# Attention's first norm: the weight multiplied straight out of PSUM, squares in place, the row's scale put on afterwards by ScalarE

## The chip, the cores and the metric

The kernel runs on one core of a Trainium2 chip. The metric is the device time of one execution in microseconds (us); lower is better. Before the change it is 8548.28 us, the median of three executions (8543.92 to 8550.57).

## The reference

Two layers are computed on `x`, fp32 of 8 images x 192 channels x 64 x 64 pixels. The first is a selective scan over the image in four directions, with a norm and a projection at its end; the second is window attention in 8 x 8 windows with a top-16 mask, followed by a feed-forward part. Cut to the part that matters here:

```python
# end of layer 0
y = layernorm2d(y, ln_w, ln_b)
y = grn(y, grn_gamma, grn_beta)
x = conv1x1(y, W_out)                       # 384 -> 192 channels
# start of layer 1
xs = transpose(x)                           # tokens x 192
shortcut = _layer_norm(xs, norm1_g, norm1_b)  # (x-mu)*rsqrt(var+1e-5)*g + b
qkv = windows(shortcut) @ qkv_w.T + qkv_b
...                                         # top-16 softmax in windows, proj
x2 = shortcut + out
hdn = _layer_norm(x2, norm2_g, norm2_b)
x2 = x2 + gelu(hdn @ fc1_w.T + fc1_b) @ fc2_w.T + fc2_b
```

## The kernel before

Three strands of work are laid out for each image: a *front* (projection and 3x3 convolution, `front`), the *scan* (`scan`: eight steps, each over four directions and three blocks of 128 channels) and the *window rows* (`window_row`: eight rows of windows, 512 tokens each). While image b is scanned, the front of image b+1 and the window rows of image b-1 run beside it. At the start there is only a front and a scan without window rows; at the end eight window rows run after the last scan.

The order on each engine is not the order of the code. Every piece of work is handed to a planner, `plan(engine, cost, function, r=..., w=...)`, with a cost in ns, what it reads and what it writes. `Plan.order` (L146) then runs a list scheduler over all of them twelve times, with ranks by due time, keeps its best outcome, and emits the instructions of PE (TensorE), ScalarE (ACT), VectorE (DVE), GpSimd (POOL) and the transfer queue SP in that order. A changed piece of work or cost therefore gives a new order everywhere. Lanes (`plan.lane`) keep the order in which pieces of one strand may take buffers.

PSUM has two banks for the scan's `nb` and six that all else shares (`l_ps`, L450, handed out by `bank()`, L466). Each unit of the scan takes three of the six for its gates (`g`, matmuls at L673; read by ScalarE's Abs at L730 and by VectorE's multiplies at L722, L737 and L739) and four more for its outputs (read at L828 and L833). The window rows take theirs from the same six.

A window row begins thus. `zg`, the scan's result for 512 tokens, is loaded (L1027) and scaled by ScalarE (L1032). For each half `t2` of the row a bank `pz` gets two blocks of 128 tokens x 192 channels by the matmuls of L1047 (`tokens`); the mean over the channels has been taken out of `w_out` beforehand, so only the scale remains of the norm. ScalarE squares each block out of PSUM with the sum along the row accumulated into `ss`, and writes the squares themselves, which nobody reads, into `s0` (L1053). GpSimd turns the sum into the mean plus 1e-5 (L1062); `rsqrt` (L469) makes 1/sqrt of it with Ln, Exp and Square on ScalarE (L478 to L480) and three steps on GpSimd (L483 to L485). Then VectorE multiplies each block in PSUM by the row's scale `ss` and by the weight `n1_g` and writes it to `s0` in SBUF (L1069). That ends the use of `pz`. The bias of the norm has been folded into later weights.

`s0` is transposed by PE (L1012), copied to `sT` (L1020) and projected to q, k and v (L1093, L1131); it is read once more when the residual is added (L1368), a multiply-free twin of the new instruction in shape: 128x384 out of PSUM with a second operand from SBUF. Further names used below: the top-16 search (L1234 to L1238), the exps and shares of the softmax (L1276, L1288), the second norm's scaling (L1411), fc1 (L1443, L1447), its bias (L1454), gelu over a whole row with an activation-table load before and after (L1463, L1464), and fc2 (L1477).

Of the kernel before, what the change touches and what calls it, by code (L numbers as in the profile page):

```python
# [25 lines left out]
AF = mybir.ActivationFunctionType  # L26
ALU = mybir.AluOpType
# [4 lines left out]
P = 128  # L32
B, DM, H, W = 8, 192, 64, 64
# [16 lines left out]
def view(ap, dims, offset=0):  # L50

    return bass.AP(ap.tensor, ap.offset + offset, [ap.ap[0]] + dims)
# [231 lines left out]
def tile_ss2d_then_window_attention(ctx: ExitStack, tc: tile.TileContext, a: dict, out: bass.AP):  # L284
# [6 lines left out]
    nc = tc.nc  # L291
# [7 lines left out]
    def load(name, src=None, rows=None):  # L299

        nonlocal n_loads
        src = a[name] if src is None else src
        shape = list(src.shape)
        t = const.tile([rows or shape[0]] + shape[1:], F32, tag=name, name=name)
        if rows:
            nc.vector.memset(t[HALF:rows], 0.0)
        queues[n_loads % 2].dma_start(t[0 : shape[0]], src)
        n_loads += 1
        return t
# [18 lines left out]
    n1_g = load("n1_g", a["n1_g"].partition_broadcast(P))  # L328
# [41 lines left out]
    with tc.tile_pool(name="prep", bufs=2) as prep, tc.tile_pool(name="prep_ps", bufs=2, space=PSUM) as prep_ps:  # L370
# [12 lines left out]
        for n, pair in enumerate(PAIRS):  # L383
            for k, (d, _) in enumerate(pair):
                w = w_g2[64 * k : 64 * k + 64, n * P : (n + 1) * P]
# [51 lines left out]
        for ci in range(2):  # L437
            w = w_f1[:, ci, :]
# [15 lines left out]
    plan = Plan()  # L454
    vec = lambda n: (n / 0.96 + 69, 88)
# [10 lines left out]
    def bank(name="lp"):  # L466
        return Held(l_ps, [P, 512], name, tag="lp")

    def rsqrt(v, key, shape, name, gain=1.0):  # L469

        c = (gain / 2) ** (1 / 3)
        if gain not in log_c:
            log_c[gain] = blank(f"log_c{len(log_c)}", [P, 1], math.log(c))
        r, sq = Held(small, shape, name + "_r"), Held(small, shape, name + "_q")
        plan("ACT", tiny, lambda: nc.scalar.activation(r(), v(), AF.Ln), r=[key], w=[r])  # L478
        plan("ACT", tiny, lambda: nc.scalar.activation(r(), r(), AF.Exp, scale=-0.5, bias=log_c[gain]), w=[r])
        plan("ACT", tiny, lambda: nc.scalar.activation(sq(), r(), AF.Square), r=[r], w=[sq])  # L480

        def newton():
            nc.gpsimd.tensor_mul(v(), v(), sq())  # L483
            nc.gpsimd.tensor_scalar(v(), v(), -1.0, 3.0 * c * c, ALU.mult, ALU.add)
            nc.gpsimd.tensor_mul(v(), v(), r())  # L485

        plan("POOL", (750.0, 60.0), newton, r=[r, sq], w=[key])
# [516 lines left out]
    def window_row(b, g, z, sc, bb):  # L1004
# [30 lines left out]
        s0 = Held(lpool, [P, NT, DM], "s0", bufs=2)  # L1035
        for t2 in range(2):
            pz = bank()
            ss = Held(small, [P, 2], "ss")
            for k in range(2):

                def tokens(t2=t2, k=k, pz=pz):
                    tt = 2 * t2 + k
                    for ct in range(CT):
                        for w in range(2):
                            half = pz()[64 * w : 64 * w + 64, k * DM : (k + 1) * DM]
                            tok = view(zg(), [[CH, 64]], ct * 512 + 2 * tt + w)
                            nc.tensor.matmul(half, lhsT=tok, rhs=w_out[:, ct, :], start=ct == 0, stop=ct == CT - 1)  # L1047

                plan("PE", mm(3, DM), tokens, r=[zg], w=[(pz, k), (s0, "room")])
                plan(  # L1050
                    "ACT",
                    (430.0, 100.0),
                    lambda k=k, pz=pz, ss=ss, t2=t2: nc.scalar.activation(  # L1053
                        s0()[:, 2 * t2 + k, :], pz()[:, k * DM : (k + 1) * DM], AF.Square, accum_out=ss()[:, k : k + 1]
                    ),
                    r=[(pz, k)],
                    w=[(s0, t2), (ss, k)],
                )
            plan(
                "POOL",  # L1060
                tiny,
                lambda ss=ss: nc.gpsimd.tensor_scalar(ss(), ss(), 1.0 / DM, 1e-5, ALU.mult, ALU.add),  # L1062
                w=[ss],
            )
            rsqrt(ss, ss, [P, 2], "ss")

            def scaled(t2=t2, pz=pz, ss=ss):
                for k in range(2):
                    nc.vector.scalar_tensor_tensor(  # L1069
                        s0()[:, 2 * t2 + k, :],  # L1070
                        pz()[:, k * DM : (k + 1) * DM],
                        ss()[:, k : k + 1],
                        n1_g,
                        ALU.mult,
                        ALU.mult,
                    )

            plan("DVE", (650.0, 90.0), scaled, r=[pz, ss], w=[(s0, t2)])
            yield
        plan.lane = 7  # L1080
        two_blocks(sT, "sT", s0)
# [5 lines left out]
        for tt in range(NT):  # L1087
            pq = bank()

            def projected(tt=tt, pq=pq):  # L1090
# [11 lines left out]
                r=[pq],  # L1102
                w=[(qk, tt)],
# [5 lines left out]
                r=[(qk, tt)],  # L1109
                w=[pq],  # L1110
# [7 lines left out]
                r=[pq],  # L1118
                w=[(nn, tt)],
# [4 lines left out]
        for p2 in range(2):  # L1124
            pv = bank()

            def values(p2=p2, pv=pv):
# [18 lines left out]
                r=[pv],  # L1146
                w=[(v, p2)],
# [13 lines left out]
            w=[nn],  # L1161
# [12 lines left out]
        for k in range(4):  # L1174
            pt = bank()

            def turn(k=k, pt=pt):
# [10 lines left out]
                r=[pt],  # L1188
                w=[(qkT[k // 2], k % 2)],
# [26 lines left out]
        for r in range(3):  # L1216
# [5 lines left out]
                r=[pas[r]],  # L1222
                w=[(at, r)],
            )
        for r in range(3):
# [21 lines left out]
            def mask(rng=rng, less=less):  # L1247
# [9 lines left out]
            part = lambda rng=rng: at()[:, rng, :]  # L1257
# [6 lines left out]
                w=[(at, r)],  # L1264
# [5 lines left out]
                r=tops,  # L1270
                w=[(down, r)],
# [24 lines left out]
        for r in range(3):  # L1296
            pt = bank()

            def turn(r=r, pt=pt):
# [11 lines left out]
                r=[pt],  # L1311
                w=[(at, r)],
# [18 lines left out]
        for w in range(2):  # L1331
# [7 lines left out]
                r=[po[w]],  # L1339
                w=[("oT", w)],  # L1340
# [6 lines left out]
        for t2 in range(2):  # L1347
            pp = bank()
            two = slice(2 * t2, 2 * t2 + 2)
            stats, mv, sd = Held(small, [P, 2, 6], "stats"), Held(small, [P, 2, 2], "mv"), Held(small, [P, 2], "sd")  # L1350

            def projected(t2=t2, pp=pp):
# [20 lines left out]
                r=[pp, s0],  # L1373
                w=[(x2, t2)],
            )

            def moments(t2=t2, stats=stats, mv=mv):
# [9 lines left out]
                r=[mv],  # L1387
                w=[sd],
# [8 lines left out]
                r=[mv],  # L1397
                w=[less_m],
# [5 lines left out]
                r=[sd],  # L1404
                w=[less_m],
# [31 lines left out]
        for m2 in range(NM // 2):  # L1437
# [12 lines left out]
            for k in range(2):  # L1450
# [6 lines left out]
                    r=[ph[k]],  # L1457
                    w=[(hd, 2 * m2 + k)],
# [10 lines left out]
        for ci in range(2):  # L1469
# [4 lines left out]
            def narrowed(ci=ci, pf=pf, n=n):  # L1474
# [22 lines left out]
                r=[pf],  # L1497
                w=[ot],
# [13 lines left out]
    def windows(b, z, made):  # L1512
        for g in range(NG):
            yield from window_row(b, g, z, *made[b])
# [107 lines left out]
```

## Time and profile before

| | |
|---|---|
| median of three executions | 8548.28 us |
| the profiled execution | 8535.73 us, of which the span is 8533.9 us |
| granted TensorE clock, mean | 0.818 |
| busy PE / DVE / ACT / POOL | 83% / 74% / 64% / 68% |
| L1053, squares (ACT), 128x192 | 256 times, 325 ns mean, 83.1 us busy |
| L1069, scaled multiply (DVE), 128x192 | 256 times, 407 ns mean, 92.1 us busy |
| L1368, residual add (DVE), 128x384 | 128 times, 547 ns mean, 69.8 us busy |

The page of the profile is that of one execution. "Busy" is the time in which an engine has an instruction under way; where two of one kind overlap it is less than count times mean. In the rows of groups, `out<-in` gives tiles by the program's names without buffer numbers (`s` is `s0`, `lp` a bank), then the shape, the count, the busy time, the mean duration of one, and the idle time of the engine just before such instructions with what ended most of it. `L1069` is line 1069 of the kernel. The chain of work that ended last is followed back from the last instruction, at each step to what released it.

### The profile page before, as it was taken

The numbers are of one execution on the slowest core, as the hardware profiler recorded it, in microseconds if no ns is written. First come the engines' busy times: TensorE is split into PE (matmuls) and PEld (weight loads), VectorE is DVE, ScalarE is ACT, GpSimd is POOL, SyncE is SP. The second block draws the span as 40 slices with busy tenths as digits, with TensorE's granted clock in tenths as the row PEclk, the third lists the DMA queues.
The fourth block names the chain that finished last, engine by engine and source line by source line (L and its number), as shares of the span: only waits on it lengthen the run. The fifth ranks groups of instructions, "written<-read, shape, count | busy, mean of one in ns | idle before, by whom it ended". The sixth has DMA issues, their size and how long they took to land.

```text
span 8533.9 us, 147117 instructions
## 1 busy us (share of the span) xinstructions
PE 7066.1 (83%) x51224; PEld 3646.0 (43%) x51224; DVE 6350.5 (74%) x15549; ACT 5425.1 (64%) x12281; POOL 5839.1 (68%) x5918
## 2 busy tenths in 40 slices
PE   5787688888888888788888888888888888888887
PEld 2333344444444444444444444444444444444554
DVE  1366778888787887877788777787788888888543
ACT  1354447676676757665676656766577656667776
POOL 0377877778777677777777667676777777777311
PEclk8887578887888889786888888977778878778888
DMA  6776154212533155213531134311211111111110
GB/s 176 188 194 160 49 137 120 79 43 72 137 98 78 36 138 133 70 47 85 147 95 51 42 88 132 107 39 46 56 44 41 46 52 53 40 41 42 26 23 12
DMA packets 1037949, 695.69 MB, mean 82 GB/s; under 512 B 704116, under 2 KB 860215, under 8 KB 1037207
## 3 DMA queue, kind: packets, MB, share of 16 engines
q1 hardware_dynamic: 1035830, 684.99, 30.1%
q8 instruction: 406, 6.65, 0.3%
q14 instruction: 337, 2.75, 0.1%
q10 hardware_dynamic: 1376, 1.30, 0.1%
HBM read 453.43 MB, written 232.67 MB: 80 GB/s over the span
## 4 chain that ended last, share of the span: by engine, by line
PE 37%; DVE 17%; ACT 17%; POOL 13%; DMA 9%; issue 5%; SPq 1%; POOLq 0%; DVEq 0%; ACTq 0%
PE g L673 10%; PE lp L560 4%; PE lp L1477 4%; PE lp L1443 3%; POOL pr L791 3%; DMA strip<-pad 3%; DMA zg<-z 3%; ACT at L1276 2%; PE lp L1093 2%; PE lp L1047 2%; ACT at L1288 2%; POOL ab L761 2%; POOL pr L776 2%; POOL dx L842 2%; DVE pr L737 2%
## 5 line engine op out<-in xcount | busy, mean ns | idle before, releaser
L673 PE MATMUL g<-xe,w_g 32*128 32x512 f32 x3648 | 1301.1, 780 | 316.3 <-DVE dx L828 115.5
L673 PE MATMUL g<-xo,w_g 32*128 32x512 f32 x3648 | 1263.1, 774 | 238.5 <-DVE dx L828 65.1
L761 POOL TENSOR_TENSOR ab<-ab 128x512 f32<-128x512 f32 x672 | 863.2, 1285 | 407.3 <-ACT ab L730 401.4
L791 POOL TENSOR_TENSOR pr<-pr,rr 128x512 f32<-128x512 f32 x672 | 873.0, 1299 | 340.9 <-ACT rr L774 307.0
L776 POOL TENSOR_TENSOR pr<-pr 128x512 f32<-128x512 f32 x672 | 872.9, 1299 | 316.5 <-DVE pr L737 204.5
L730 ACT ACTIVATE ab<-g 128x512 f32<-128x512 f32 x1344 | 770.8, 593 | 320.6 <-PE nb L673 166.2
L560 PE MATMUL lp<-strip,w_cv 128*32 128x256 f32 x9216 | 687.2, 442 | 288.4 <-DMA strip<-pad 264.5
L780 POOL TENSOR_TENSOR pr<-pr 128x512 f32<-128x512 f32 x672 | 869.9, 1295 | 24.3
L842 POOL TENSOR_TENSOR dx<-dx,hu 128x512 f32<-128x512 f32 x576 | 739.0, 1291 | 183.6 <-DVE hu L833 172.3
L673 PEld LDWEIGHTS g<-xe,w_g 32*128 32x128 f32 x3648 | 461.1, 220 | 895.4 <-DVE dx L828 242.5
L673 PEld LDWEIGHTS g<-xo,w_g 32*128 32x128 f32 x3648 | 441.8, 219 | 804.5 <-issue 202.7
L772 ACT ACTIVATE rr<-nb,eps 128x512 f32<-128x512 f32 x672 | 460.0, 685 | 486.5 <-DVE nb L769 423.9
L787 DVE SCALAR_TENSOR_TENSOR nb<-nb,rr 128x512 f32<-128x512 f32 x672 | 465.2, 692 | 338.5 <-ACT rr L774 337.2
L1477 PE MATMUL lp<-hd,w_f 128*64 128x256 f32 (+1 forms) x2304 | 603.9, 500 | 75.2 <-ACT hd L1463 61.0
L795 DVE SCALAR_TENSOR_TENSOR nb<-nb,pr 128x512 f32<-128x512 f32 x672 | 464.8, 692 | 195.6 <-POOL pr L791 191.8
L560 PEld LDWEIGHTS lp<-strip,w_cv 128*32 128x32 f32 x9216 | 314.0, 123 | 669.3 <-issue 357.6
L850 POOL TENSOR_TENSOR y<-y,dx 128x512 f32<-128x512 f32 x384 | 596.4, 1561 | 3.1
L769 DVE TENSOR_TENSOR nb<-nb,ab 128x512 f32<-128x512 f32 x672 | 465.2, 692 | 154.9 <-POOL ab L761 125.8
L752 ACT ACTIVATE nb<-nb 128x512 f32<-128x512 f32 x672 | 396.8, 591 | 221.5 <-DVE pr L737 111.3
L840 POOL TENSOR_TENSOR y<-hu,dx 128x512 f32<-128x512 f32 x192 | 248.8, 1303 | 406.6 <-DVE hu L833 406.2
L833 DVE TENSOR_TENSOR hu<-g,hid 128x512 f32<-128x512 f32 x768 | 519.9, 678 | 8.0 <-PE g L673 6.4
L673 PE MATMUL nb<-xe,w_g 32*128 32x512 f32 x672 | 497.9, 829 | 8.0 <-DVE hid L802 7.9
(201 smaller groups left out, 17042.9 us busy)
## 6 DMA issues: line engine op xcount, KB each, us to landing
strip<-pad SPq DMA_DIRECT2D x1152, 132.0 KB
xd<-xsT SPq DMA_DIRECT2D x384, 256.0 KB
pad<-xin SPq DMA_DIRECT2D x192, 264.0 KB
xs<-st SPq DMA_DIRECT2D x192, 256.0 KB
xsT<-sn SPq DMA_DIRECT2D x192, 256.0 KB
xd<-xs SPq DMA_DIRECT2D x192, 256.0 KB
x<-xs SPq DMA_DIRECT2D x64, 768.0 KB
z<-y SPq DMA_DIRECT2D x64, 768.0 KB
```

Source lines behind the costliest of these rows:

```text
L560: nc.tensor.matmul(pc()[q * RG : (q + 1) * RG, k * 256 : (k + 1) * 256].rearrange("p (h w) -> p h w", h=4), lhsT=w_cv[:, ct, q, dx, :], rh ...
L673: nc.tensor.matmul(dst, lhsT=w[rows, col : col + P], rhs=xp[rows, :], start=True, stop=True)
L730: lambda r=r: nc.scalar.activation(ab()[:, r, :], g[r](), AF.Abs),
L761: plan("POOL", gp(512), lambda: nc.gpsimd.tensor_add(ab()[:, 0, :], ab()[:, 0, :], ab()[:, 1, :]), w=[ab])
L769: plan("DVE", vec(512), lambda: nc.vector.tensor_add(nb(), nb(), ab()[:, 0, :]), r=[ab], w=[nb])
L776: plan("POOL", gp(512), lambda: nc.gpsimd.tensor_add(one(), one(), pr()[:, 1, :]), r=[(pr, 1)], w=[(pr, 0)])
L780: lambda: nc.gpsimd.tensor_add(one(), one(), pr()[:, 2, :]),
L791: plan("POOL", gp(512), lambda: nc.gpsimd.tensor_mul(one(), one(), rr()), r=[rr], w=[(pr, 0)])
L833: lambda: nc.vector.tensor_mul(like(hu(), d), like(pu(), d), state(d, ct)),
L842: plan("POOL", gp(512), lambda: nc.gpsimd.tensor_add(dx(), dx(), hu()), r=[hu], w=[dx])
L850: nc.gpsimd.tensor_add(y, y, dx().rearrange("p (c i) -> p i c", c=CH))
L1477: nc.tensor.matmul(dst[:, at : at + rhs.shape[-1]], lhsT=lhsT, rhs=rhs, **flags)
```

## The change

Three things change in each of the 128 halves. One VectorE instruction multiplies both blocks, 384 columns, by the weight as soon as the matmuls are done and writes them to `s0`. ScalarE's two squares, now one piece of work, write over the blocks in PSUM rather than into `s0`, after that multiply, and the bank is free from then on. When the scale is there, ScalarE multiplies the two blocks in `s0` by it, in place (`Copy` with a scale read from `ss`), where VectorE multiplied out of PSUM by scale and weight. The steps that make the scale are the same.

```diff
                 plan("PE", mm(3, DM), tokens, r=[zg], w=[(pz, k), (s0, "room")])
-                plan(
-                    "ACT",
-                    (430.0, 100.0),
-                    lambda k=k, pz=pz, ss=ss, t2=t2: nc.scalar.activation(
-                        s0()[:, 2 * t2 + k, :], pz()[:, k * DM : (k + 1) * DM], AF.Square, accum_out=ss()[:, k : k + 1]
-                    ),
-                    r=[(pz, k)],
-                    w=[(s0, t2), (ss, k)],
-                )
+            two = slice(2 * t2, 2 * t2 + 2)
+            plan(
+                "DVE",
+                vec(2 * DM),
+                lambda two=two, pz=pz: nc.vector.tensor_mul(
+                    s0()[:, two, :],
+                    pz()[:, 0 : 2 * DM].rearrange("p (k m) -> p k m", k=2),
+                    n1_g.unsqueeze(1).to_broadcast([P, 2, DM]),
+                ),
+                r=[pz],
+                w=[(s0, t2)],
+            )
+
+            def squares(pz=pz, ss=ss):
+                for k in range(2):
+                    part = pz()[:, k * DM : (k + 1) * DM]
+                    nc.scalar.activation(part, part, AF.Square, accum_out=ss()[:, k : k + 1])
+
+            plan("ACT", (860.0, 100.0), squares, w=[pz, ss])
             plan(
                 "POOL",
                 tiny,
@@
             rsqrt(ss, ss, [P, 2], "ss")
 
-            def scaled(t2=t2, pz=pz, ss=ss):
+            def scaled(t2=t2, ss=ss):
                 for k in range(2):
-                    nc.vector.scalar_tensor_tensor(
-                        s0()[:, 2 * t2 + k, :],
-                        pz()[:, k * DM : (k + 1) * DM],
-                        ss()[:, k : k + 1],
-                        n1_g,
-                        ALU.mult,
-                        ALU.mult,
-                    )
-
-            plan("DVE", (650.0, 90.0), scaled, r=[pz, ss], w=[(s0, t2)])
+                    part = s0()[:, 2 * t2 + k, :]
+                    nc.scalar.activation(part, part, AF.Copy, scale=ss()[:, k : k + 1])
+
+            plan("ACT", (600.0, 120.0), scaled, r=[ss], w=[(s0, t2)])
             yield
```

In the changed file the multiply is L1054, the squares L1066 and the scaling L1080; lines below it are four higher than before.

## The prediction

> **What bounds the kernel now.** I began with the page's busy shares and its chain of work that ended last:
>
> ```profile
> PE 7066.1 (83%) x51224; PEld 3646.0 (43%) x51224; DVE 6350.5 (74%) x15549; ACT 5425.1 (64%) x12281; POOL 5839.1 (68%) x5918
> ...
> PE 37%; DVE 17%; ACT 17%; POOL 13%; DMA 9%; issue 5%; SPq 1%; POOLq 0%; DVEq 0%; ACTq 0%
> ```
>
> No engine is full and no engine owns the chain: it hops between PE, VectorE, ScalarE and GpSimd. Dividing chain share by busy share, 17/64 = 0.27 of a microsecond of ScalarE work lies on the chain and 17/74 = 0.23 of one of VectorE. Averages hide stages, so next the busy times by stretch (columns: stretch, length, then busy of PE, PEld, DVE, ACT, POOL), first the stage with scans and window rows together, then the tail after the last scan:
>
> ```profile
> 1180.00:7980.00 6800.00, 5763.17 (x41382) 2991.78 (x41382) 5476.79 (x13364) 4565.26 (x10453) 5066.73 (x5114) 0.83 0.28 74
> 7982.00:8534.00 552.00, 456.31 (x3927) 280.70 (x3926) 234.06 (x1153) 399.31 (x1059) 96.48 (x263) 0.88 0.09 20
> ```
>
> In the mixed stage PE is busy 85%, VectorE 81%, ScalarE 67%. In the tail VectorE falls to 42% and PE (83%) with ScalarE (72%) sets the pace. Third, the groups of instructions, for the lines concerned and their nearest kin (busy, mean ns | idle before):
>
> ```profile
> L1288 ACT ACTIVATE at<-at,rden 128x64 f32<-128x64 f32 x1536 | 385.5, 338 | 71.5 <-DVE rden L1282 67.7 <-DVE top L1234 2.9
> ...
> L1411 ACT ACTIVATE xn<-x,less_m,sd 128x192 f32<-128x192 f32 x256 | 125.1, 538 | 43.9 <-POOL less_m L1403 43.6
> ...
> L1069 DVE SCALAR_TENSOR_TENSOR s<-lp,ss,n_g 128x192 f32<-128x192 f32 x256 | 92.1, 407 | 38.0 <-POOL ss L485 37.7
> L1053 ACT ACTIVATE s<-lp 128x192 f32<-128x192 f32 x256 | 83.1, 325 | 92.8 <-PE lp L1047 91.9
> L1368 DVE TENSOR_TENSOR x<-lp,s 128x384 f32<-128x384 f32 x128 | 69.8, 547 | 35.4 <-PE lp L1356 34.9
> ```
>
> Last, the view of line 1069, which today releases the bank pz: who waits for it.
>
> ```profile
> who waited for it (us, times):
>   PEld g L673: 34.6, 37
>   PE g L673: 7.5, 9
> ```
>
> The scan's matmuls (L673) need three free banks of the same six. With L1443, L1131, L1207, L514, L1424 and L1093 in that list, waits that end with this bank's release sum to 50 us. From the starts and ends in the trace, over the 128 halves (64 window rows x 2), the bank is held 20.4 us in the mean from its first matmul to the end of L1069; 13.9 us of that (median 11.7) lies between the last accumulator read of L1053 and the start of L1069, while seven tiny steps on GpSimd (L1062, L483, L484, L485) and ScalarE (L478, L479, L480) make the scale.
>
> **What the Trainium skill says.** "Perfetto Trace Analysis", Optimization Strategy: the same gap repeating on the engine that should be saturated can mean that there isn't enough PSUM for the next tile. The trace agrees in kind: 476 us of PE idleness in the mixed stage stands just ahead of L673 matmuls (261.0 + 215.3 in the groups of that stretch), mostly until VectorE is done with earlier banks. "PSUM — Partial Sum Buffer", PSUM bank collisions: two engines may not touch one bank and quadrant at once, reads included; so the multiply and the squares cannot overlap, in place or not. No run here tries it. The same page, Engine vs sequencer instructions: ScalarE and VectorE queues are strict FIFO; nothing I saw in the trace contradicts it.
>
> **The change part by part.**
> 1. *VectorE.* 256 scaled multiplies of 192 columns go (92.1 us busy), 128 multiplies of 384 columns come; L1368 is their twin in shape and memories (69.8 us). Saving 22.3 us x 0.23 = **-5 us**.
> 2. *ScalarE, new copies.* The built order has 256 more ScalarE instructions. "ScalarE: Activation LUTs", What ACT_TABLE_LOAD costs, prices an ACTIVATE at 186 + 0.833 N ns, plus 93 per pointer operand, less 93 when back to back. That is 332 for L1288 (one pointer, 64 columns; median 334) and 532 for L1411 (two pointers, 192; 535), so I trust it: 439 for one pointer and 192 columns. A pair then occupies 439 + 346 = 785 ns; 128 pairs 100 us. Bounds by busy time per instruction: 256 x 0.251 (L1288) = 64 and 256 x 0.489 (L1411) = 125 us. Taken: 100 x 0.27 = **+27 us**. In-place squares cost what L1053 costs (L1108 squares 384 PSUM columns in place in 492 ns, its copy L1101 to SBUF takes 481).
> 3. *A moved wait.* VectorE no longer waits for the scale (37.7 us, 31.5 of it in the tail) but for the tokens' matmuls; its twin waits 34.9 us for its own. I put nothing: one idle time stands in for the other, beside a VectorE that in the mixed stage has 19% of slack; without that cover it would be 35 x 0.23 = 8 us. But the squares, which wait 91.9 us for PE, now wait for the multiply too: 0.55 us plus its turn on a VectorE that is 81% busy, 0.7 us by guess. Queued behind squares in the built order are most often the Abs of the next gates (L730), the Exp of the scan (L774) and the copies of xT; GpSimd's ab and PE's next bank wait for those. Between 0 and 128 x 1.25 = 160 us of ScalarE; I take 30 us, as most squares come late enough to be ready, x 0.27 = **+8 us**.
> 4. *The bank.* Hold shrinks from 20.4 us to 4.2 (its matmuls) plus about 1.25 and 1.0 (squares with accumulator reads) and idle turns, say 8: 12 us x 128 = 1500 us of bank time, 3.5% of six banks over 7350 us. Worth between 0 (the next bank in the rotation is as late) and more than the 50 us of direct waits, since PE's 476 us before L673 include indirect ones. Taken: half the direct ones, **-25 us**. What is late next: VectorE's reads of gates (L828, L722), which end most of the other waits.
> 5. *The order.* The plan is recomputed, so all engines' orders change. Counting matmuls on PE up to the last scan matmul: before, 53 window rows had finished L1477 and 55 had L1093; after, 54 and 56. The tail so holds one leftover row less. Tail rows come every 56 us (starts of the gelu, L1463: 8124.6, 8180.1, 8236.9, 8292.6). Inside the scans a row costs less: the first scan, without rows, ran from 292 to 1119 us (827), scans two and three with some eight rows each ended at 2096 and 3073 (977 each), so (977 - 827)/8 = 19 us; comparing scans of about 6 and 8 rows (923 and 977) gives nearer 30. Taken 25: 25 - 56 = **-31 us**. Bounds: 0, if the extra row stretches the scans by as much as it shortens the tail, and -37.
>
> SP's transfers, PE's and GpSimd's instruction counts stay. s0 has two buffers as before.
>
> Sum: -5 + 27 + 8 - 25 - 31 = **-26 us**, against the profiled execution: 8535.7 - 26 = 8510. It ran 12.5 us under the median shown, 8548.3, so I forecast **8522 us**, 0.3% faster.
>
> **Rivals.**
> *ScalarE becomes the late engine* (slower). In tail rows and between scans the new copies stand behind gelu with its table loads (5.3 us) and exps (2 us a group), and the transposes of s0 (L1012) wait for them where they waited for VectorE. Of 130 us of added ScalarE time and blocking, my gains of 61 are used up when 61/130 = 47% lies on the chain instead of 27%. At 75% it is +98 - 61 = +37: 8585 us. For it: ScalarE waits often release GpSimd and VectorE (L787 waits 337 us for L774). Against: ScalarE idles a third of the mixed stage.
> *Banks were the true limit.* Then freed bank time pays indirectly: a quarter of the 476 us, 119 us in place of 25: 8522 - 94 = 8428 us. For it: the repeating waits at L673. Against: PE is already busy 85% there.
> *Hidden anyway.* The new order merely moves the row, the bank was never the last wait, and copies fit into ScalarE's idle third: 8548 us. This is also the case in which early release doesn't do what it says, because the multiply or squares are themselves late and hold the bank about as long.
> *The reshuffle.* Scans with like work differ by some 15 us beyond what rows explain; over seven, 15 x 2.6 = 40 us of scatter either way, on top of all cases.
>
> **How the numbers follow.** Forecast 0.45 (own range 8495 to 8531), banks the limit 0.13 (8400 to 8490), hidden 0.15 (8531 to 8565), ScalarE late 0.27 (8565 to 8610). Differences below 0.2%, 17 us, are about what a measurement of this kernel can't tell from none. Faster: 0.45 + 0.13 = 0.58; same 0.15; slower 0.27. Leaving out about 1 in 10 at each side: 8460 to 8590.
>
> **What would show it.** After: L1054 near 547 ns x128 on VectorE; copies at line 1080 near 440 ns, about 100 us busy; waits on bank release ended by the squares (L1066) below 50 us; first matmul to last square about 8 us; tail from the last scan's end (595 us before: 7938.7 to 8533.9) some 45 to 55 us shorter, everything ahead of it some 25 longer; PE idle before L673 in the mixed stage below 476. I am wrong if ScalarE waits for VectorE at the squares exceed 100 us, if L1012 waits for the copies by tens of microseconds, or if the scans stretch by more than the tail shrinks.

## The result, and the profile after

The changed kernel takes 8486.5 us (median of four executions, 8477.6 to 8488.0) beside 8546.1 us for the kernel before: ratio 0.9929, 95% interval 0.9912 to 0.9946, some 60 us faster, where 26 were forecast. The page of its profiled execution (8477.55 us, span 8475.7) has nearly the same shares; ScalarE's part of the chain has grown:

```profile
PE 7074.7 (83%) x51224; PEld 3638.9 (43%) x51224; DVE 6356.4 (75%) x15421; ACT 5520.5 (65%) x12537; POOL 5838.5 (69%) x5918
...
PE 35%; ACT 19%; DVE 17%; POOL 13%; DMA 9%; issue 5%; SPq 1%; POOLq 0%; DVEq 0%; ACTq 0%
```

ScalarE has 95 us more work and a larger part of the chain; VectorE's busy time is unchanged to 6 us although it issues 128 instructions fewer. The gain is not in anyone's busy time. It is in PE's idle time (the span less PE's busy time), 1467.8 us before and 1401.0 after. To see where, I cut both executions at the end of the first scan and the end of the last (the last L833 of each image) and took the busy times of these stretches (columns: stretch, length, busy of PE, PEld, DVE, ACT, POOL, then PE's granted clock). Before:

```profile
1119.20:7938.70 6819.50, 5787.89 (x41405) 3000.59 (x41404) 5495.71 (x13307) 4547.60 (x10394) 5096.60 (x5130) 0.82 0.28 76
7938.70:8533.90 595.20, 490.80 (x4222) 300.78 (x4222) 257.88 (x1277) 433.60 (x1151) 107.72 (x283) 0.88 0.09 20
```

After:

```profile
1129.30:7899.40 6770.10, 5834.87 (x41793) 3019.81 (x41791) 5531.19 (x13322) 4669.68 (x10722) 5113.03 (x5158) 0.83 0.28 76
7899.40:8475.70 576.30, 443.13 (x3833) 271.54 (x3831) 228.57 (x1134) 406.08 (x1077) 90.32 (x255) 0.87 0.09 20
```

The first scan, without window rows, is 10 us longer. The mixed stage is 49 us shorter although it does 47 us more of PE's work: PE is busy 86.2% of it, not 84.9%. The tail is 19 us shorter and holds 48 us less of PE's work. 10 - 49 - 19 = -58, the whole difference of the two spans. The granted clock is almost the same (0.819 after and 0.818 before, in the mean over the span).

The groups that were touched (busy, mean ns | idle before):

```profile
L1080 ACT ACTIVATE s<-s,ss 128x192 f32<-128x192 f32 x256 | 101.4, 448 | 25.5 <-POOL ss L485 25.2
...
L1066 ACT ACTIVATE lp<-lp 128x192 f32<-128x192 f32 x256 | 80.8, 316 | 35.3 <-DVE s L1054 31.1
...
L1054 DVE TENSOR_TENSOR s<-lp,n_g 128x384 f32<-128x384 f32 x128 | 69.9, 547 | 49.8 <-PE lp L1047 49.8
```

VectorE's new multiply is 22 us cheaper than the scaled multiplies were (69.9 us beside 92.1), but two lines of the top-16 mask took 29 us more, so that its total did not fall. Before:

```profile
L1251 DVE COPY_PREDICATED at<-less,neg 128x512 f32<-128x512 uint8 x192 | 189.7, 988 | 6.6
L1248 DVE TENSOR_TENSOR less<-at,kth 128x512 uint8<-128x512 f32 x192 | 165.0, 859 | 0.3
```

After:

```profile
L1255 DVE COPY_PREDICATED at<-less,neg 128x512 f32<-128x512 uint8 x192 | 209.0, 1089 | 6.6
L1252 DVE TENSOR_TENSOR less<-at,kth 128x512 uint8<-128x512 f32 x192 | 174.8, 910 | 0.1
```

And who waits for the line that now releases the bank, the squares:

```profile
who waited for it (us, times):
  POOL ss L1072: 122.2, 36
  PEld g L673: 39.3, 38
  PE g L673: 13.3, 12
  PEld lp L1447: 7.3, 4
```

From starts and ends in the trace the bank is held 9.7 us in the mean, from its first matmul to the last accumulator read of the squares (20.4 before, to the end of L1069). Yet the scan's matmuls wait no less for its release: 39.3 + 13.3 = 52.6 us against 34.6 + 7.5 = 42.1.

### The profile page after: what moved, and what is told of

It is laid out like the page before. It is cut to its first block, busy times and chain, and to the rows that moved or that the text cites. A ratio compares the mean times of both kernels' runs of the same rounds, so it can differ in the third digit from the quotient of the medians.

```text
span 8475.7 us, 147154 instructions
## 1 busy us (share of the span) xinstructions
PE 7074.7 (83%) x51224; PEld 3638.9 (43%) x51224; DVE 6356.4 (75%) x15421; ACT 5520.5 (65%) x12537; POOL 5838.5 (69%) x5918
## 4 chain that ended last, share of the span: by engine, by line
PE 35%; ACT 19%; DVE 17%; POOL 13%; DMA 9%; issue 5%; SPq 1%; POOLq 0%; DVEq 0%; ACTq 0%
PE g L673 10%; PE lp L560 5%; PE lp L1481 4%; POOL pr L791 3%; ACT at L1292 3%; DMA strip<-pad 3%; ACT at L1280 3%; PE lp L1447 2%; PE lp L1047 2%; DMA zg<-z 2%; POOL ab L761 2%; POOL pr L776 2%; PE lp L1097 2%; DVE pr L737 2%; POOL dx L842 2%
## 5 line engine op out<-in xcount | busy, mean ns | idle before, releaser
L673 PE MATMUL g<-xo,w_g 32*128 32x512 f32 x3648 | 1316.4, 791 | 268.5 <-DVE dx L828 80.6
L673 PE MATMUL g<-xe,w_g 32*128 32x512 f32 x3648 | 1295.1, 777 | 270.7 <-DVE dx L828 81.7
L673 PEld LDWEIGHTS g<-xo,w_g 32*128 32x128 f32 x3648 | 465.3, 223 | 850.5 <-issue 217.7
L673 PEld LDWEIGHTS g<-xe,w_g 32*128 32x128 f32 x3648 | 452.3, 218 | 841.5 <-DVE dx L828 205.8
L833 DVE TENSOR_TENSOR hu<-g,hid 128x512 f32<-128x512 f32 x768 | 519.5, 679 | 6.6 <-PE g L673 5.0
L673 PE MATMUL nb<-xe,w_g 32*128 32x512 f32 x672 | 498.0, 830 | 16.0 <-DVE hid L802 15.8
```

The costliest lines, as they stand in the source:

```text
L673: nc.tensor.matmul(dst, lhsT=w[rows, col : col + P], rhs=xp[rows, :], start=True, stop=True)
L833: lambda: nc.vector.tensor_mul(like(hu(), d), like(pu(), d), state(d, ct)),
```

## The experiments

All ratios are to the kernel before, run on the same chip with it. "Mixed" and "tail" are the stretches of the profiled execution as cut above. "Own length" is what `Plan.order` reckons for the order that it emits (`self.length`, from its own model of costs): no measurement, but it can be had without the chip.

| kernel | operations | bank in the plan | own length | median us | ratio (95%) | mixed | tail |
|---|---|---|---|---|---|---|---|
| before | before | to the scaled multiply | 7982 | 8536 to 8546 | 1 | 6820 | 595 |
| n1 | before | the same | 7975 | 8555.1 | 1.0012 (1.0003 to 1.0020) | 6818 | 614 |
| n2 | before | the same | 8063 | 8602.6 | 1.0081 (1.0066 to 1.0096) | 6857 | 637 |
| e1 | after | order of before | 7982 | 8594.4 | 1.0055 (1.0040 to 1.0070) | 6860 | 606 |
| e2 | after's, copies first | to the copies | 7975 | 8567.4 | 1.0021 (1.0013 to 1.0029) | 6845 | 572 |
| e5 | after | to the copies | 8033 | 8566.2 | 1.0037 (1.0025 to 1.0049) | 6809 | 637 |
| x2 | after | to the copies | 8022 | 8546.5 | 1.0016 (1.0006 to 1.0026) | 6825 | 604 |
| x3 | after | to L1072 | 7941 | 8527.2 | 0.9993 (0.9983 to 1.0002) | 6780 | 635 |
| after | after | to the squares | 7886 | 8486.5 | 0.9929 (0.9912 to 0.9946) | 6770 | 576 |
| n3 | after | to the squares | 7920 | 8472.3 | 0.9923 (0.9906 to 0.9939) | 6765 | 582 |
| n4 | after | to the squares | 7923 | 8487.7 | 0.9944 (0.9930 to 0.9959) | 6771 | 590 |
| x1 | after + plain copies | order of after | 7886 | 8484.7 | 0.9947 (0.9930 to 0.9964) | 6778 | 582 |
| x4 | after + second multiply | order of after | 7886 | 8478.0 | 0.9934 (0.9915 to 0.9952) | 6781 | 580 |
| e3 | scale on VectorE | to the squares | 7954 | 8577.4 | 1.0033 (1.0020 to 1.0046) | 6891 | 566 |

**e1: the new operations in the old order.** The planner sees before's pieces and costs; only what they issue differs.

```diff
-                plan("ACT", (430.0, 100.0), lambda ...: nc.scalar.activation(s0 ..., pz ..., AF.Square, accum_out=...),
-                    r=[(pz, k)], w=[(s0, t2), (ss, k)])
+                def squares(k=k, pz=pz, ss=ss, t2=t2):
+                    if k == 0:
+                        return
+                    nc.vector.tensor_mul(s0()[:, 2 * t2 : 2 * t2 + 2, :], ...)   # both blocks by n1_g
+                    for j in range(2):
+                        part = pz()[:, j * DM : (j + 1) * DM]
+                        nc.scalar.activation(part, part, AF.Square, accum_out=ss()[:, j : j + 1])
+                plan("ACT", (430.0, 100.0), squares, r=[(pz, k)], w=[(s0, t2), (ss, k)])
...
-                    nc.vector.scalar_tensor_tensor(...)
+                    nc.scalar.activation(part, part, AF.Copy, scale=ss()[:, k : k + 1])
```

> Theory A, the early release of the bank pays on the chip, whatever the order: the new operations are put into the order of before (the multiply and both squares where the second square stood, the copies where VectorE's scaled multiply stood), so the bank is free early but nothing is re-planned. A expects 20 to 40 us less than before (8505 to 8525). Theory B, the gain comes from the new order (the planner packs one more row ahead of the last scan and hits a luckier sequence): no gain here, 8535 to 8575, as the copies cost ScalarE 100 us of work and no order is better. Theory C, lighter VectorE: 5 us less at most.

It is 0.55% slower than before, more than any of the theories allowed (8594 us; B went to 8575). On the chip the bank was held 7.0 us in the mean, less even than in after. So an early release on the chip that the order doesn't know of is worth less than what the operations cost there. The squares now wait for a multiply that VectorE's order hasn't made room for (group of the squares in e1; with after's order the same wait is 31.1 us):

```profile
L1060 ACT ACTIVATE lp<-lp 128x192 f32<-128x192 f32 x256 | 80.6, 315 | 135.1 <-DVE s L1053 130.6
```

That took away theory A as I had put it ("whatever the order").

**e2: the same work, the bank held until the scale.**

```diff
-                    nc.scalar.activation(part, part, AF.Square, accum_out=ss()[:, k : k + 1])
+                    nc.scalar.activation(s0()[:, 2 * t2 + k, :], part, AF.Square, accum_out=ss()[:, k : k + 1])
...
-            plan("ACT", (600.0, 120.0), scaled, r=[ss], w=[(s0, t2)])      # s0 -> s0
+            plan("ACT", (600.0, 120.0), scaled, r=[pz, ss], w=[(s0, t2)])  # pz -> s0
+            plan("DVE", vec(2 * DM), lambda ...: nc.vector.tensor_mul(s0 ..., s0 ..., n1_g ...), w=[(s0, t2)])
```

> Same 2 squares, 2 copies with a scale and 1 multiply of 384 columns for each half, but the copies read PSUM once the scale is there and the multiply then runs in SBUF, so the bank is held as long as before (20 us in the mean, where after holds 9.7). Planned anew. Theory A: the gain is lost, 8545 to 8590. Theory B: any new order lands within 40 us of 8517, with no tie to the bank. Theory C: as after, 8490.

8567 us: the gain is lost, as A expects. It is no clean test, since the multiply, with both operands now in SBUF, takes longer (876 ns in the mean, 547 in after) and VectorE waits 96.4 us for the copies:

```profile
L1075 DVE TENSOR_TENSOR s<-s,n_g 128x384 f32<-128x384 f32 x128 | 111.0, 876 | 96.6 <-ACT s L1066 96.4
```

**e3: the scale put on by VectorE, bank free early.**

```diff
-                    nc.scalar.activation(part, part, AF.Copy, scale=ss()[:, k : k + 1])
+                    nc.vector.tensor_scalar(part, part, ss()[:, k : k + 1], None, ALU.mult)
...
-            plan("ACT", (600.0, 120.0), scaled, r=[ss], w=[(s0, t2)])
+            plan("DVE", (400.0, 90.0), scaled, r=[ss], w=[(s0, t2)])
```

> As after, but the scale is put on in SBUF by VectorE (two multiplies by a per-row scalar) in place of ScalarE's two copies: the bank is free early and ScalarE carries 100 us less, VectorE some 50 us more. Theory A with my price of ScalarE work (27 us for the whole): 8465 to 8485, a little better than after. If ScalarE's copies are hidden anyway: 8490 or somewhat more. If VectorE is what limits: 8500 or more.

It is 0.33% slower than before (8577 us), which fits only the last of the three. I had put VectorE's new work at 50 us; it is 178, while the planner allows 0.4 us for a pair (group in e3):

```profile
L1080 DVE TENSOR_SCALAR s<-s,ss 128x192 f32<-128x192 f32 x256 | 178.1, 742 | 48.3 <-POOL ss L485 48.1
```

Why these are slow is told at the end. That the mixed stage is the longest of all, 6891 us, follows a VectorE pair that runs a microsecond over its plan and waits for the scale besides; how much of the loss is each, and how much the order, I can't tell apart.

**n1 to n4: other orders of the same two kernels.** One cost in the plan is changed, nothing else.

```diff
n1: -                    (430.0, 100.0),                            + (450.0, 100.0),
n2: -            plan("DVE", (650.0, 90.0), scaled, ...)            + (700.0, 90.0)
n3: -            plan("ACT", (860.0, 100.0), squares, ...)          + (900.0, 100.0)
n4: -            plan("ACT", (600.0, 120.0), scaled, ...)           + (785.0, 120.0)
```

> The kernel before with one planner estimate changed (a square priced 450 ns, not 430): same operations and same bank hold, another order. It measures the scatter of re-planning. Theory A: within 20 us of 8546. Theory B: can be off by 30 to 60 us either way.

> The kernel before with the other estimate changed (VectorE's pair of scaled multiplies priced 700 ns, not 650): the second measure of the scatter. Theory A: within 20 us of 8546. Theory B: may be as low as 8490 or as high as 8590.

> After with one planner estimate changed (the pair of squares priced 900 ns, not 860): same operations, another order. Theory A (early release pays, whatever the order): 8470 to 8505. Theory B (after drew a lucky order): back towards the others, 8515 to 8575.

> After with the pair of copies priced 785 ns in the planner, as it takes on the chip, not 600: same operations, another order. Theory A: 8470 to 8505. Theory B: 8515 to 8575.

A new order alone moves before by +0.1% and +0.8%, as much as the whole effect under study; n2 (8602.6 us) fell outside what either theory expected. But three orders of after lie within 0.21% of each other (0.9923, 0.9929, 0.9944), and none of before's comes near them. So after did not draw a single lucky order; theory B, as I had put it, falls.

**e5 and x2: the plan alone holds the bank.** Operations and costs are after's. The copies are said to read the bank, so the planner doesn't give it out until they are done. On the chip the squares release it as before.

```diff
-            plan("ACT", (600.0, 120.0), scaled, r=[ss], w=[(s0, t2)])
+            plan("ACT", (600.0, 120.0), scaled, r=[pz, ss], w=[(s0, t2)])
```

x2 has n3's cost of 900 ns for the squares besides.

> After's operations, but the planner is told that the bank is in use until the copies are done, so the order is made with as little room in the banks as before had (on the chip the squares still release it). Theory A in the form that the room in the plan is what pays: 8530 to 8570. Theory B: anywhere from 8490 to 8570. If neither the bank nor the order counts but the operations alone: as after, 8487.

> The kernel in which the planner holds the bank until the copies, with the pair of squares priced 900 ns, not 860: another order of the same kind. If room in the plan is the cause: 8530 to 8600, away from after's 8472 to 8488. If that kernel's 8566 was an unlucky order: 8470 to 8510.

e5 alone fits both theories, since B allowed up to 8570. x2 separates them: if e5 had been an unlucky order, x2 should have come back to 8470 to 8510. In both every instruction is the same as in after and the time from first matmul to last accumulator read, 10.35 us in e5, differs little from after's 9.7. Only the order differs, and with it goes the whole gain: 1.0037 and 1.0016 against 0.9923 to 0.9944. Mean against mean, 1.0027 - 0.9932 = 0.95%, some 81 us. The stretches of e5 (mixed, tail) beside those of after:

```profile
1114.10:7922.90 6808.80, 5852.43 (x41513) 3028.34 (x41512) 5506.93 (x13231) 4629.12 (x10608) 5102.47 (x5131) 0.82 0.28 76
7922.90:8559.70 636.80, 493.74 (x4114) 298.80 (x4114) 250.91 (x1228) 448.71 (x1191) 96.52 (x282) 0.85 0.08 19
```

Its mixed stage is 39 us longer than after's and leaves one leftover row more: its tail has PE busy 494 us, not 443, and is 60 us longer. The granted clock differs a little between orders (0.8115 in e5, 0.8175 in after, medians). It is not the whole cause: n4 runs at 0.8145 and x2 at 0.815, and they are 59 us apart. It may be a part. Over the 61 executions of before that were run beside these kernels on three chips, time falls by 24 to 47 us for each 0.01 of granted clock; e5 and x2 have 0.004 less in the mean than after, n3 and n4, so some 10 to 20 of the 81 us could be the clock's (an estimate from these slopes). Nor do the two lose alike: against after's profiled execution PE is busy 69 us and idle 15 us longer in e5, busy 21 us and idle 44 us longer in x2.

Two orders against three, where a nudge moves before by 69 us, would be thin evidence by itself. The planner's own lengths in the table make it firmer. Take the nine kernels whose operations are before's or after's and whose order was planned for them (before, n1, n2, after, n3, n4, e5, x2, x3): from after, n3 and n4 (7886 to 7923) to x2 and e5 (8022 and 8033) and n2 (8063) these lengths put them in nearly the order in which the chip puts them. The fast and the slow orders thus differ in the plan already. What stays thin is that a nudge alone can lengthen a plan as much (n2), and only two orders were made with the hold. The planner misses e3 (7954), whose VectorE work it prices far too low.

**x3: a shorter hold in the plan.**

```diff
                 lambda ss=ss: nc.gpsimd.tensor_scalar(ss(), ss(), 1.0 / DM, 1e-5, ALU.mult, ALU.add),
+                r=[pz],
                 w=[ss],
```

> After's operations; the planner holds the bank a little past the squares, until GpSimd's first step on the sums (L1072), and not until the copies. A dose between none (8472 to 8488) and full (8566). If the time in the plan counts: 8490 to 8540. If only the scatter of orders is at work: anywhere.

It lies between, as a dose should, but not evenly: its mixed stage (6780) is after's, and nearly its whole loss is in the tail (635). PE idles no longer in it than in after (1396.2 us, 1401.0) but is busy 67 us longer, and its own length (7941) is closer to the fast orders than to the slow. One order can't tell a dose from the scatter of tails, which go from 566 to 637 in these runs.

**x1 and x4: what ScalarE's and VectorE's time is worth.** After's order is kept; the planner knows nothing of the additions.

```diff
x1:                  nc.scalar.activation(part, part, AF.Copy, scale=ss()[:, k : k + 1])
   +             for k in range(2):
   +                 nc.scalar.activation(s0()[:, 2 * t2 + k, :], s0()[:, 2 * t2 + k, :], AF.Copy)
x4: -                lambda two=two, pz=pz: nc.vector.tensor_mul(...)
   +                 lambda two=two, pz=pz: [nc.vector.tensor_mul(...) for _ in range(2)]
```

> After, in its own order, with a plain copy of each block of s0 onto itself behind the scaled copies: 256 more ScalarE instructions, some 80 us, which the planner doesn't know of. It prices ScalarE's time. My price (0.27 of it on the chain): 22 us more than after (8509). Hidden: 8490. ScalarE late (0.75 or more): 8547 and up.

> After, in its own order, with the multiply by the weight issued twice: 128 more VectorE instructions, some 70 us, not known to the planner; the bank and the squares wait 0.5 us longer each time. It prices VectorE's time. At my price of 0.23: 16 us more than after (8503). If VectorE is what limits: 8530 or more.

The group that x1 added:

```profile
L1083 ACT ACTIVATE s<-s 128x192 f32<-128x192 f32 x256 | 77.4, 352 | 0.0
```

77.4 us more of ScalarE cost 0.9947 - 0.9929 = 0.18%, 15 us, with intervals that overlap: nothing up to about half of it is on the chain, so my 0.27 stands as possible, and a ScalarE that is late at 0.75 (58 us) is out. x4's second multiply adds 71 us (141.2 busy, not 69.9) for 0.05%, 4 us, with intervals that allow anything from nothing to some 26 us.

## Why the prediction was right, and which steps failed

The direction and the range (8460 to 8590) held; the size was off by more than two, and the reason that carried most of it was not the one that I gave. That the sign came out right is in part luck: the two terms that made it, the bank and the order, both failed in how they were to work.

1. *VectorE* (-5): the twin's duration was right to the nanosecond (547), and so were the 22 us saved in these two lines. But VectorE's total rose by 6 us, as L1251 and L1248 took 29 us more, so the saving never arrived. The price of VectorE's time was not measurable either: 71 us more in x4 cost 4 us.
2. *ScalarE's copies* (+27): 448 ns against 439 worked out from the Trainium skill's formula that the prediction quotes, 101.4 us busy against 100. The duration was right; x1 puts their price between nothing and not quite twice mine.
3. *The moved wait* (+8) had the wrong sign for ScalarE. The squares do wait 31.1 us for VectorE, where I took 30, but I had them come on top of the 91.9 us for which L1053 waited for PE, and they came in its place: ScalarE's idle time before the squares fell from 92.8 us to 35.3. It is VectorE that now waits for the tokens' matmuls, 49.8 us where L1069 waited 37.7 for the scale. That 31 is near 30 is therefore luck, and only the new order gives it: in e1, with the old one, ScalarE's idle time before the squares is 135.1 us.
4. *The bank* (-25) failed in its mechanism. The hold fell to 9.7 us, 8 expected, but waits ended by the release did not fall below 50 us: with all the lines that wait for L1066's banks they are about 70. PE's idle time ahead of L673's gate matmuls in the mixed stage went from 264.4 + 215.3 = 480 us to 244.8 + 221.4 = 466 only. What the early release buys is room in the plan, shown by e5 and x2, and it acts as a better order, not as shorter waits of this bank's next users.
5. *The order* (-31) had the right sign and the wrong places. One row more is done ahead of the last scan's end, as counted. But I let it cost 25 us there and save 56 in the tail. In fact the mixed stage came out 49 us shorter with that row in it, and the tail only 19 shorter: its rows come every 57.2 us in the mean, not 55.8 (seven gaps, 10 us; the copies are 1.6 us of ScalarE work a row), and the first row of the last image lies 157 us behind the scan's end where it lay 186. The failed step is "in the scans the row costs 25"; my count of instructions on PE could show that one row moves, not that everything between would also be packed more tightly. Nor is that row what pays: n4 has only 53 rows through fc2 at the last scan matmul, like before, and is fast; x2 has 54, like after, and is not.

Of the rivals, "ScalarE late" is ruled out by x1, "hidden anyway" by the result and n3, n4. "Banks the true limit" had the right subject and too large a number (8428), and its indirect path was the waits at L673, which hardly moved. "The reshuffle" was put at 40 us either way; for one order of before it is 69 us (n2).

What stays open is how the room turns into time. In the mixed stage PE's idle time (length less busy) fell from 1031.6 us to 935.2, and in the tail it rose from 104.4 to 133.2. No single wait shrank by as much; PE's waits in the mixed stage, before,

```profile
PE g L673 <- DVE dx L828: 127.7, 83, 16.1
PE g L673 <- DVE lx L722: 94.4, 57, 15.8
PE lp L560 <- DMA strip<-pad: 74.8, 35, 5.8
```

and after,

```profile
PE g L673 <- DVE dx L828: 109.2, 90, 10.8
PE g L673 <- DVE lx L722: 78.2, 50, 9.5
PE lp L560 <- DMA strip<-pad: 56.6, 28, 4.9
```

each give back 16 to 19 us, and some others grow (L673 for VectorE's L737: 26.9 to 42.7). That is what a generally tighter order looks like, but I have not isolated a place in it.

## What to carry to other kernels

Where a planner or scheduler writes the order, a change to how long a buffer is held is a change to the plan's room first; test it by holding the buffer in the plan alone, with the same instructions, before crediting the hardware. Nudge a cost or two on both sides to learn how much a new order moves by itself (up to 0.8% here): one re-planned run against another proves little. If the planner reckons a length for its order, compare that first: for nine of these kernels it told the fast orders from the slow without the chip, and it failed where a cost was far off (e3). And work moved to an engine with idle time is cheap only where nothing waits at its ends: x1's copies, which the order did not know of, cost some 15 us (nothing to 36), while in e1 the change's instructions in the old order cost 0.55%, with the squares waiting 130.6 us for the multiply.

## What the runs showed of the hardware that I had not expected

Some VectorE instructions whose tensors all lie in SBUF take longer while GpSimd works. In e3 a scalar multiply of 192 columns takes from 271 to 1615 ns. The 95 that hardly overlap a GpSimd instruction of over 1 us take 313 ns in the mean, the 119 that lie in such instructions for nine tenths of their time or more 1182, and all of the 88 longer than 1 us end 0.115 to 0.12 us (5th to 95th in the hundred) after such a GpSimd instruction has ended. In the timeline of e3 (start us, us, instruction) VectorE's three in a row end at 1439.95, 0.12 us after the last of GpSimd's three:

```profile
1435.82 1.28 POOL L776 TENSOR_TENSOR pr<-pr 128x512 f32<-128x512 f32 x1
1435.91 4.04 DVE L1080 TENSOR_SCALAR s<-s,ss 128x192 f32<-128x192 f32 x3
1437.07 1.53 POOL L850 TENSOR_TENSOR y<-y,dx 128x512 f32<-128x512 f32 x1
1438.56 1.27 POOL L780 TENSOR_TENSOR pr<-pr 128x512 f32<-128x512 f32 x1
```

The multiply by the weight is stretched too when both operands are in SBUF (e2's L1075: 506 to 1890 ns, mean 876), and not when one of them is in PSUM (L1054: 507 to 559; before's L1069: 365 to 419). The kernel before had it already: L1248 takes 663 ns where it hardly overlaps such a GpSimd instruction and 1180 where half of it or more does, L1251 738 and 1514. It is not so for every instruction in SBUF alone: before's L1281 (a sum, 632 to 687 ns) and L1234 (a search for the largest eight, 174 to 230) keep their times.

The Trainium skill ("GPSIMD Engine Reference", Specifications) says that GpSimd's SBUF interfaces are shared with VectorE and that VectorE instructions with two SBUF inputs or in a two-port mode contend. L1248 and L1075, with two SBUF inputs, agree and give the size, and so do L1281 and L1234, with one tensor read. e3's multiply reads one tensor, so it would have to run in such a mode, which no run here shows. With GpSimd busy 69% of the span, a scale put on in SBUF belongs on ScalarE here (448 ns, 433 to 521), as the change has it.
